# Layer norm, attention and a gated FFN on one core: the home and the request times of the down weights, and the order of work where two batches of the FFN meet

## The chip, the core and the metric

The kernel runs on one core of a Trainium2 chip. A core has five engines that run their own instruction queues side by side and meet only through semaphores: TensorE (PE in the profile; its weight loads are PEld), VectorE (DVE), ScalarE (ACT), GpSimd (POOL) and SyncE (SP). Transfers between the main memory and the on-chip memory are asked for by an instruction in the queue of SP, ACT or POOL; an instruction that waits holds up everything behind it in its queue. The metric is the time of one execution on the device, in microseconds (us). The kernel before was run three times: 1219.32, 1221.62 and 1223.13 us, so its median is 1221.62 us.

## The reference

```python
x = L0_attn_x                                  # (4, 512, 512), float32
xn = layernorm(x)
s = attention(xn)                              # 16 heads of 128, causal, with biases
g = silu(((silu((xn @ gate_w.T) * gate_s) * ((xn @ up_w.T) * up_s)) @ down_w.T) * down_s)
return x + s * g
```

There are four batches of 512 rows with 512 columns. `gate_w` and `up_w` are 1408 by 512, `down_w` is 512 by 1408. All data are float32. The weights of the FFN hold only the values -1, 0 and 1.

## The kernel before

The kernel has two stages. The first is the layer norm and the attention; its result for each batch and each tile of 128 rows goes to scratch tensors in main memory (`acc`), the last four of them from a tile `a_last` on chip (line 506). The second stage is the FFN with the final product (`ffn_exact`, lines 780 to 1106). A flag that is found during the first stage says whether the FFN weights are exact in the short form that TensorE multiplies; if so, `ffn_exact` runs. Each activation is split into a high and a low part (`hi`, `lo`), and each weight is multiplied with both.

The FFN cuts the 1408 inner columns into eleven chunks (`f` = 0 to 10). One chunk of one batch is a unit; the units go batch by batch, chunk by chunk. A unit is computed in one of two ways. In the plain way (`plain`) a gate product of 8 matmuls is followed by an up product of 8 matmuls, 512 columns each. The first four chunks of batch 0 and the first of batch 1 are plain (`PLAIN = (4, 1, 0, 0)`). All others use `seven` (lines 927 to 1002): a scheme of the Strassen kind, with seven products of 4 matmuls of 256 columns in place of the eight that two outputs need. It takes sums of the weights, made in the first stage and kept in main memory (`sum`), and sums of x, made on VectorE by `sums_of` (lines 806 to 853). `sums_of` has 13 additions on VectorE and 4 copies on ScalarE; it is a generator, and `advance(n)` lets the next n additions go into the queues. The four results are called t1 to t4, each as a high and a low part.

A unit is a list of (time, function). The functions of two neighbouring units are merged by their times: a unit starts every 7 steps and its functions run from step 0 to step 19. So the tail of a unit (`at9`, `at10`, `at11`, ...) is mixed with the head of the next (`at0`, `at1`, `at3`, ...). `run(upto)` issues everything due before a step. The names used below are: `at0` and `at1` are the two gate products (tiles px and py), with a ScalarE copy s1 after the first and a VectorE addition after the second; `at3` adds a product into px after s1 has been copied, then ScalarE copies u2 and applies silu; `at5` is the product s1 t1 into pz; `at6` adds into px again after u2 has been copied; `at8` is the VectorE addition c (tile `c22`) of pz and u3; `at9` and `at11` add the last products into px and pz. `at11` must wait until `at8` has read pz.

When the first unit of a new batch has been issued, the old batch gets its down product: for each of four tiles of 128 rows, 22 matmuls of 512 columns (`Down.add`, line 1025), and then `leave`: VectorE multiplies (line 766), ScalarE applies silu (767), VectorE multiplies by the attention's result and adds x (768, 769), SP stores. The down tiles have two PSUM buffers, so that the third tile starts only when line 766 of the first has run.

Buffers come from pools that are laid out on chip one behind the other in the order in which they are opened. The FFN's pools lie where the attention's pools lay. The first tile written in a pool waits for all users of everything that lay in that pool's whole range. Before, the order was: x sums (`tp`), the streamed weights (`fw`), the down weights (`wdp`), the inner activations (`hp`), the small temporaries (`fp`), the tail's inputs (`fa`). The range of `wdp` held, among others, a part of `a_last`.

All weights of the FFN are asked for by GpSimd's queue in program order (`load`, line 863; `load_down`, line 859). In each of the eleven units of batch 0 the unit's own weights come first and then one tile of down weights (line 1077).

Of the kernel before, what the change touches and what calls it, by code (L numbers as in the profile page):

```python
# [13 lines left out]
AF = mybir.ActivationFunctionType  # L14
# [29 lines left out]
def kernel(  # L44
# [69 lines left out]
    with ExitStack() as at:  # L114
# [464 lines left out]
        with tc.manual_schedule():  # L579
# [177 lines left out]
                    inexact = any_of(low)  # L757
            last = (NG - 1, B - 1)
            zs[last].append(attend(H - 1, pt, v_of[last], False))
            for t in range(NT):  # L760
                project_out(*last, t, zs[last])
            warm_up(LINGER)
# [17 lines left out]
    def ffn_exact():  # L780
        with ExitStack() as ff:

            tp = ff.enter_context(tc.tile_pool(name="tp", bufs=1))
            fw = ff.enter_context(tc.tile_pool(name="fw", bufs=3))
            wdp = ff.enter_context(tc.tile_pool(name="wdp", bufs=1))
            hp = ff.enter_context(tc.tile_pool(name="hp", bufs=NF + 1))
            fp = ff.enter_context(tc.tile_pool(name="fp", bufs=2))
            fa = ff.enter_context(tc.tile_pool(name="fa", bufs=3))
            ps_x = ff.enter_context(tc.tile_pool(name="ps_x", bufs=3, space=PSUM))
            ps_y = ff.enter_context(tc.tile_pool(name="ps_y", bufs=1, space=PSUM))  # L790
            ps_z = ff.enter_context(tc.tile_pool(name="ps_z", bufs=2, space=PSUM))
# [65 lines left out]
            def load_down(k):  # L857
                wd[k] = wdp.tile([P, D], F32R, name=f"wd{k}", tag=f"wd{k}")
                nc.gpsimd.dma_start(out=wd[k], in_=down_w[k])
# [66 lines left out]

            def seven(b, f):

                (b11, _), (b21, b22) = blk[b]
                t1, t2, t3, t4 = t_of[b]  # L930
                g = load(gate_w[f], [P, ND, P], "wg")
# [64 lines left out]
                def at17():  # L996
                    next(made["left"], None)

                return [
                    (0, at0), (1, at1), (3, at3), (5, at5), (6, at6), (8, at8), (9, at9),  # L1000
                    (10, at10), (11, at11), (13.5, at13), (15.5, at14), (17.5, at16), (19, at17),
                ]

# [35 lines left out]
            with tc.manual_schedule():  # L1039
                events, sums = [], sums_of(0)  # L1040

                def run(upto):

                    events.sort(key=lambda e: e[0])
                    while events and events[0][0] < upto:
                        events.pop(0)[1]()

                def advance(n=99):
                    for _ in range(n):
                        next(sums, None)  # L1050

                units = [(b, f) for b in range(B) for f in range(NF)]
                for k, (b, f) in enumerate(units):
                    at_ = 7 * k
                    if b > 0 and f == 1:

                        run(at_)
                        for e in [e for e in events if e[2] == k - 2]:
                            events.remove(e)
                            e[1]()  # L1060
                        if b == 1:
                            sums = sums_of(b)
                            advance()
                        for t in range(NT):
                            Down(b - 1, t).add(range(NF)).leave()
                            if t + 3 < NT:
                                load_tail(b - 1, t + 3)
                    if f < PLAIN[b]:
                        unit = plain(b, f)
                        if b == 0:  # L1070
                            advance((6, 3, 2, 1)[f])
                    else:
                        if b == 0 and f == PLAIN[b]:
                            advance()
                        unit = seven(b, f)
                    if b == 0:
                        load_down(f)
                    if 0 < b < B - 1 and f == 2:
                        sums = sums_of(b + 1)
                    if 0 < b < B - 1 and 2 <= f < 9:  # L1080
                        unit = sorted(
                            unit + [(2.5, lambda: advance(1)), (5.5, lambda: advance(1))],
                            key=lambda e: e[0],
                        )
                    events += [(at_ + n, what, k) for n, what in unit]
                    run(at_ + 7)
                    if f == NF - 1:
                        for t in range(3):
                            load_tail(b, t)
                last = B - 1  # L1090
                n0 = 7 * len(units)
                d0 = Down(last, 0).add(range(0, 4))
                run(n0 + 3)
                d0.add(range(4, 7))
                run(n0 + 6)
                d0.add(range(7, NF - 1))
                run(n0 + 99)
                d1 = Down(last, 1).add(range(NF - 1))
                d0.add([NF - 1]).leave()
                load_tail(last, 3)  # L1100
                d1.add([NF - 1]).leave()
                Down(last, 2).add(range(NF)).leave()
                h_ = D // 2
                d3 = Down(last, 3, slice(0, h_)).add(range(NF))
                d3.leave()
                Down(last, 3, slice(h_, D), nc.scalar, d3.o).add(range(NF)).leave()
# [175 lines left out]
```

## Time and profile before

| what | value |
|---|---|
| median of three runs | 1221.62 us |
| the profiled execution | 1221.51 us |
| span of its instructions | 1219.7 us |
| TensorE busy | 1194.8 us, 98% of the span |
| VectorE busy | 944.8 us, 77% |
| ScalarE busy | 599.8 us, 49% |
| GpSimd busy | 447.3 us, 37% |
| mean granted TensorE clock | 0.993 of full speed |
| FFN, from its first matmul to the end | 960.0 to 1219.7 us |
| main memory, read and written | 193 GB/s over the span |

The profile is of one execution. Its time is 1.8 us longer than the span between its first and its last instruction. "Busy" counts the time in which an engine had an instruction in hand; matmuls are pipelined, so that a small share of missing busy time can be the part that matters. "Granted clock" is the share of full speed that TensorE was allowed. A line such as "A <- B: 5.4, 1, 5.4" means that A waited for B 5.4 us in total, once, for 5.4 us at the longest.

### The profile page before, as it was taken

The page shows a single profiled execution, that of the slowest core. Times are in us where ns is not written, and L with a number is a line of the kernel's source. Part 1 is how long each engine was busy: PE and PEld are TensorE (multiplying, and loading weights), DVE is VectorE, ACT ScalarE, POOL GpSimd, SP SyncE. Part 2 cuts the span into 40 slices and gives each one's busy share as a digit, 9 for nine tenths or more (in the row PEclk, how much of TensorE's full clock was granted, in tenths as well). Part 3 has the DMA queues.
Part 4 walks back from the last instruction along what each step waited for, and adds up shares of the span by engine and source line. Part 5 has one row for each costly group of instructions (what it writes and reads, how often), then busy time and mean ns, then how long its engine had stood idle before and what let it go on. Part 6 is the DMA issues. An engine that isn't in the chain of part 4 may idle for free. (4 is left out here: it accounts for less than half of the span.)

```text
span 1219.7 us, 20216 instructions
## 1 busy us (share of the span) xinstructions
PE 1194.8 (98%) x6486; PEld 1040.9 (85%) x6486; DVE 944.8 (77%) x2496; ACT 599.8 (49%) x1449; POOL 447.3 (37%) x611
## 2 busy tenths in 40 slices
PE   9999999999999999999999999999999898999997
PEld 8888888888888888888888888888888697989896
DVE  7987777888778878787878787777777566859574
ACT  6654444554454445454545454455444252636362
POOL 3312342444244335333533354234322370525240
PEclk9999999999999999999999999999999898999999
DMA  4464456756676667666666666656555793959591
GB/s 162 144 188 151 144 177 194 216 173 213 200 215 191 210 202 227 191 206 201 201 199 190 199 206 205 208 184 183 173 156 165 249 334 98 290 155 290 147 272 55
DMA packets 133042, 236.75 MB, mean 194 GB/s; under 512 B 14912, under 2 KB 58688, under 8 KB 132928
## 3 DMA queue, kind: packets, MB, share of 16 engines
q1 hardware_dynamic: 77040, 140.15, 36.5%
q10 hardware_dynamic: 29520, 53.40, 14.7%
q0 software_dynamic: 26368, 41.82, 12.4%
q8 instruction: 54, 0.88, 0.3%
q14 instruction: 60, 0.49, 0.1%
HBM read 150.51 MB, written 84.80 MB: 193 GB/s over the span
## 5 line engine op out<-in xcount | busy, mean ns | idle before, releaser
L378 POOL TENSOR_SCALAR p<-p,rtot 128x512 f32<-128x512 f32 (+3 forms) x256 | 135.2, 547 | 566.3 <-DVE rtot L375 542.2
L372 ACT ACTIVATE p<-p,nmax 128x512 f32<-128x512 f32 (+3 forms) x256 | 140.9, 552 | 143.7 <-DVE nmax L358 143.7
L290 PE MATMUL psv<-wv,xh 128*128 128x512 f32 x448 | 124.7, 400 | 0.0
L106 PE MATMUL sc<-k,q 128*128 128x512 f32 (+2 forms) x576 | 112.6, 338 | 2.0 <-DVE xl L266 1.6
L392 DVE STREAM_TRANSPOSE sq<-p 128x256 f32<-128x256 f32 x378 | 113.4, 363 | 0.0
L106 PEld LDWEIGHTS sc<-k,q 128*128 128x128 f32 x576 | 99.0, 188 | 13.8 <-ACT xh L265 1.4
L315 ACT ACTIVATE k<-psk,consts 128x512 fp32r<-128x512 f32 (+1 forms) x65 | 44.3, 681 | 106.4 <-PE psk L106 106.3
L358 DVE CUSTOM_DVE_ANT_0 p<-sc,mask 128x512 f32<-128x512 f32 (+2 forms) x192 | 96.2, 550 | 0.0
L425 ACT CAST pt<-ptr 128x640 fp32r<-128x640 f32 x126 | 85.1, 724 | 10.7 <-DMA ptr<-turn 5.9
L427 POOL TENSOR_TENSOR pt<-ptr,pt 128x640 fp32r<-128x640 f32 x53 | 83.5, 1576 | 12.8 <-ACT pt L425 9.8
L290 PEld LDWEIGHTS psv<-wv,xh 128*128 128x128 f32 x448 | 76.0, 188 | 10.0
L316 DVE SCALAR_TENSOR_TENSOR k<-psk,consts,k 128x512 fp32r<-128x512 f32 (+1 forms) x65 | 48.1, 740 | 42.7 <-ACT k L315 42.2
L427 DVE TENSOR_TENSOR pt<-ptr,pt 128x640 fp32r<-128x640 f32 x73 | 76.6, 1060 | 2.6 <-ACT pt L425 2.6
L294 PEld LDWEIGHTS psv<-wv,xl 128*128 128x128 f32 x448 | 68.4, 188 | 9.5
L1025 PE MATMUL pd<-wd,hh 128*128 128x512 f32 (+1 forms) x187 | 71.6, 388 | 4.0 <-DVE o L766 4.0
L375 DVE RECIPROCAL rtot<-tot 128x1 f32<-128x1 f32 x256 | 41.4, 162 | 40.9 <-ACT p L372 34.7
L1025 PE MATMUL pd<-wd,hl 128*128 128x512 f32 (+1 forms) x187 | 71.3, 386 | 0.0
L294 PE MATMUL psv<-wv,xl 128*128 128x256 f32 x448 | 71.0, 280 | 0.0
L505 DVE TENSOR_TENSOR a<-pso,a 128x512 f32<-128x512 f32 x108 | 69.5, 684 | 1.4 <-DMA a<-acc 0.8
L315 ACT ACTIVATE q<-psq,consts 128x512 fp32r<-128x512 f32 (+1 forms) x65 | 44.2, 680 | 34.0 <-PE psq L106 33.7
L863 POOL DMA_DIRECT2D ws<-sum x78 | 41.6, 543 | 36.4 <-PE px L874 33.4
L863 POOL DMA_DIRECT2D wg<-in_gate_w x44 | 24.0, 546 | 78.2 <-PE py L874 68.1
(612 smaller groups left out, 3299.5 us busy)
## 6 DMA issues: line engine op xcount, KB each, us to landing
turn<-sq SPq DMA_DIRECT2D x63, 640.0 KB, 2.9
ptr<-turn SPq DMA_DIRECT2D x252, 160.0 KB, 5.2
acc<-a SPq DMA_DIRECT2D x124, 256.0 KB, 2.3
a<-acc ACTq DMA_DIRECT2D x108, 256.0 KB, 3.1
ws<-sum POOLq DMA_DIRECT2D x39, 384.0 KB, 4.7
wg<-in_gate_w POOLq DMA_DIRECT2D x44, 256.0 KB, 4.3
wu<-in_up_w POOLq DMA_DIRECT2D x49, 128.0 KB, 4.4
sum<-sums SPq DMA_DIRECT2D x22, 256.0 KB, 5.1
```

Source lines behind the costliest of these rows:

```text
L106: nc.tensor.matmul(ps, l, r, start=n == 0, stop=n == len(todo) - 1)
L290: nc.tensor.matmul(ps, x_[c].hi, wv[g].both[:, :, c, :], start=c == 0, stop=False)
L294: nc.tensor.matmul(ps[:, 1], x_[c].lo, wv[g].hi[:, c, :], start=False, stop=c == ND - 1)
L315: nc.scalar.activation(q.hi[:, at_], ps, AF.Identity, bias=bias[:, h : h + 1])
L358: nc.vector.tensor_tensor_reduce(out=of[t], in0=where[t], in1=add, scale=-SCALE, scalar=BIG, op0=ALU.add, op1=ALU.min, accum_out=nmax[t],)
L372: nc.scalar.activation(of[t], of[t], AF.Exp, bias=nmax[t], scale=-1.0, accum_out=tot)
L378: nc.gpsimd.tensor_scalar(of[t], of[t], rtot, 1.0, ALU.mult, ALU.mult)
L392: nc.vector.transpose(dst.rearrange("p a s i -> p s a i"), src.rearrange("p (s a i) -> p s a i", s=n, i=Q),)
L425: nc.scalar.copy(dst(pt.hi), src)
L427: on.tensor_tensor(dst(pt.lo), src, dst(pt.hi32), ALU.subtract)
L505: nc.vector.tensor_tensor(a, ps, a, ALU.add)
L1025: nc.tensor.matmul(self.ps, part, wd[f][:, self.c], start=f == 0 and part is h_.hi, stop=f == NF - 1 and part is h_.lo,)
```

## The change

Six edits, all but the first in `ffn_exact`:

1. At the end of the attention ScalarE runs one tiny activation with silu (`table(AF.Silu)`), after the last head's activations and before the last four output projections. ScalarE's function table for silu is then loaded there.
2. The pool of the down weights is opened last. So `hp`, `fp` and `fa` move down by its size, and the down weights lie behind them.
3. The down weights are asked for from the third unit of batch 0 on: one tile in the units 2 to 5, two in 6, one in 7 to 9, two in 10.
4. In the first `seven` unit of batches 0 and 1, `at5` is issued before `at3`.
5. In batch 1's x sums (`sums_of(1)`) five additions are issued ahead of batch 0's down tiles, then four behind each of the first two tiles (the third call finds nothing left), in place of all 13 ahead of the first tile.
6. Where two batches meet, `at8` of the new batch's first unit is issued ahead of the down tiles, and `at0` and `at1` of its second unit are issued between the third and the fourth down tile.

```diff
             zs[last].append(attend(H - 1, pt, v_of[last], False))
+            table(AF.Silu)
             for t in range(NT):
                 project_out(*last, t, zs[last])
...
             fw = ff.enter_context(tc.tile_pool(name="fw", bufs=3))
-            wdp = ff.enter_context(tc.tile_pool(name="wdp", bufs=1))
             hp = ff.enter_context(tc.tile_pool(name="hp", bufs=NF + 1))
             fp = ff.enter_context(tc.tile_pool(name="fp", bufs=2))
             fa = ff.enter_context(tc.tile_pool(name="fa", bufs=3))
+            wdp = ff.enter_context(tc.tile_pool(name="wdp", bufs=1))
...
-                    (0, at0), (1, at1), (3, at3), (5, at5), (6, at6), (8, at8), (9, at9),
+                    (0, at0), (1, at1), (3, at3), (2 if f == PLAIN[b] > 0 else 5, at5), (6, at6), (8, at8), (9, at9),
...
+                def at_once(which):
+                    for e in sorted(filter(which, events), key=lambda e: e[0]):
+                        events.remove(e)
+                        e[1]()
...
                         run(at_)
-                        for e in [e for e in events if e[2] == k - 2]:
-                            events.remove(e)
-                            e[1]()
+                        at_once(lambda e: e[2] == k - 2)
+                        at_once(lambda e: e[2] == k - 1 and e[1].__name__ == "at8")
                         if b == 1:
                             sums = sums_of(b)
-                            advance()
-                        for t in range(NT):
+                            advance(5)
+                        for t in range(NT - 1):
                             Down(b - 1, t).add(range(NF)).leave()
+                            if b == 1:
+                                advance(4)
                             if t + 3 < NT:
                                 load_tail(b - 1, t + 3)
...
-                    if b == 0:
-                        load_down(f)
+                    if b == 0 and f > 1:
+                        for n in range((f - 2) * NF // (NF - 2), (f - 1) * NF // (NF - 2)):
+                            load_down(n)
...
                     events += [(at_ + n, what, k) for n, what in unit]
+                    if b > 0 and f == 1:
+
+                        at_once(lambda e: e[2] == k and e[1].__name__ in ("at0", "at1"))
+                        Down(b - 1, NT - 1).add(range(NF)).leave()
                     run(at_ + 7)
```

## The prediction

> **What bounds the kernel now.** I read the page first: TensorE is busy for 98% of the span, and the FFN, which alone is changed, takes 960.0 to 1219.7 us. So only gaps in TensorE's queue, and a lowered clock behind them, can give time. Next the list of what TensorE waits for (us in total, times, longest):
>
> ```profile
> PE pg L874 <- DMA wg<-in_gate_w: 5.4, 1, 5.4
> PE pd L1025 <- DVE o L766: 4.0, 2, 3.7
> PE px L874 <- ACT s L953: 2.8, 4, 1.5
> PE pz L874 <- DVE c L949: 1.6, 2, 0.8
> ```
>
> Third, the chain of waits in order of time (start, us, what). It shows what each gap does to the matmuls behind it:
>
> ```profile
> 963.05 6.18 DMA wg<-in_gate_w
> 969.27 3.78 PE pg L874 x8
> ...
> 974.99 1.82 PE pg L874 x8
> ...
> 1025.12 13.10 PE pd L1025 x44
> ```
>
> Eight gate matmuls take 3.78 us behind the 5.4 us gap and 1.82 us when warm; 44 down matmuls take 13.10 us behind the 3.7 us gap where the first 44 took 9.98 (0.2268 each).
>
> Fourth, the timeline around each gap:
>
> ```profile
> 952.91 0.69 ACT L471 ACTIVATE z15h<-z,consts 128x512 fp32r<-128x512 f32 x1 [2.47 <-PE z L459]
> ...
> 962.53 0.53 POOL L859 DMA_DIRECT2D wd<-in_down_w  x1 [13.23 <-SPq L1278]
> 963.05 0.55 POOL L863 DMA_DIRECT2D wg<-in_gate_w  x1
> ...
> 984.31 0.36 ACT L953 COPY s<-px 128x256 f32<-128x256 f32 x1
> ...
> 1024.38 0.68 DVE L766 TENSOR_TENSOR o<-pd,ds_bc 128x512 f32<-128x512 f32 x1
> ...
> 1098.08 0.50 PE L874 MATMUL px<-xh,ws 128*128 128x256 f32 x2 [0.28 <-ACT s L953]
> ...
> 1099.61 0.50 PE L874 MATMUL pz<-xh,ws 128*128 128x256 f32 x2 [0.79 <-DVE c L949]
> ```
>
> GpSimd stands 13.23 us before the first down tile. Its semaphore waits in front of that load end at 962.0, when the last store of `a_last` (issued 959.8, 2.0 us to landing) is in: the pool of the down weights lies over `a_last`. Unit 1's gate weight is behind it in the queue, at 963.05, and lands at 969.23. At 1024.38 line 766 of the first down tile runs 8 us after its matmuls ended at 1016.3, behind 13 additions of x's sums.
>
> **What the skill says.** "TensorE: Matmul & The Clock Gate", Part 1: one idle window of about 3.4 us halves the clock, and about 3.4 us of work restores it. The trace agrees: gaps of 5.4 and 3.7 us were followed by slow matmuls, those of 1.5 us and less were not. "ScalarE: Activation LUTs", What ACT_TABLE_LOAD costs: 1283 ns and a drain of 1380. The trace has the 1283 ns but no drain: the cast ends at 963.00, the load starts at 963.01 and the silu at 964.31. "DMA: Bandwidth & Descriptors", Queues, rings and completion order: the DMA engines take turns between queues. The trace agrees: down tile, gate and up weights issued from 962.5 to 964 all landed after 5.6 to 6.2 us, beside 1.6 MB that SP asked for; those of 975 landed after 3.0 to 3.8.
>
> **The change, part by part.**
>
> *Start of the FFN (edits 1 to 4).* The first down load now stands behind unit 2's loads. So unit 1's weights no longer wait for 962.0. But the first weight of all gets a new wait: the built program lets it wait for the tiny silu, whose target lies in the range of `fw`. z15h ends at 953.60; table load 1.28 and activation 0.20 give 955.1 instead of the issue at 947.64. Behind it in GpSimd's queue are all loads of units 0 to 2. DMA moves 13 to 90 GB/s from 953.8 to 956.2, so I take 3.0 to 4.3 us to landing: 958.1 to 959.4, ahead of the gate product at 959.99. With the 6.7 us that this very load took in traffic it would be 961.8: a loss of 1.8. I take nothing. Unit 1's gate weight goes out about 957 and lands before 963.3 even at 6.2 us; it is needed at 963.7. Unit 3's must wait for GpSimd's step on up product 0 (962.9), then two loads and a down tile of 0.55 each: 964.5, landed by 970.7 at 6.2; needed at 971.0. Close; I take nothing here too.
>
> The wait for `a_last` does not vanish: the built program hands it to the first inner activation of `hp` (a ScalarE cast, about 965.2). It is over at about 962, so it is hidden by 3 us.
>
> TensorE then runs 8 products of 1.83: 960.0 + 14.65 = 974.65 for the first `seven`, where it was 982.09. That is 7.4 us earlier. What is late next is VectorE. It starts the sums at 960.17 as before, and all its work up to the first `seven` follows without a pause: six sums to 964.28 (silu now ready at 963.9, so the 0.58 us wait there goes), then per unit 1.56 from hd to hl, 0.61 on to the next, 0.69 per sum. hd of unit 1 at 968.5, of unit 2 at 972.1, of unit 3 at 975.0. Copy s1 comes 1.04 behind hh of unit 3 (as in the trace: 983.27 to 984.31), so at 976.95; the px product 0.42 later, 977.38, against 984.73. TensorE gets there at 974.65 + 3 x 0.48 = 976.1 (edit 4 brings `at5` ahead): 1.3 us of waiting, short enough for the clock. `at6` needs copy u2, 1.20 behind as before: 978.58 against 985.93. Gain 7.35; edit 4 alone is worth 0 to 0.5, since `at6` waits for u2 in either order.
>
> *Down loads (edit 3).* The same 11 issues of 0.557 us. Units with two ask GpSimd for 2.15 + 1.11 = 3.26 of a unit's 3.36 us. The seven `seven` units ask for 6.42 MB of their own (0.917 each) and 2.36 of down tiles: 8.78 MB in 23.5 us, 373 GB/s, against 340 moved in 985 to 1008, where TensorE had no load wait. The loads run up to 6 us ahead (968.2 against 974.65), so 300 GB/s will do. Cost 0; up to 2 us if that lead is used up.
>
> *Down tiles of batch 0 (edits 5, 6).* In the old clock, down starts at 1011.30 and the sums at 1015.45. Five sums at 0.69 bring line 766 of tile 0 to 18.83; the third tile needs it at 21.3. So the 3.68 us gap and the cold clock (13.10 - 9.98 = 3.1) go. From there VectorE: 766 to silu 0.71, to 768 0.66, to 769 0.73, to the next 0.61. Tile 0 done with 769 at 20.93; four sums; tile 1 at 24.21; four sums, the last one 0.8 for its copy; tile 2 at 29.66, silu 30.37, s1 copied at 31.25, sg at 32.4, tile 3's line 766 at 32.75. TensorE: 66 matmuls to 1026.28, `at0` and `at1` 0.96, 22 matmuls to 1032.24, `at5`, `at3` to 1033.2. Then `at6` wants u2, which stands behind tile 3's silu: 32.75 + 0.71 + 0.53 + 0.42 = 1034.4. It was 1041.11. Gain 6.7, with 1.2 us still waited. Bounds: 5 if VectorE slips another 1.7; 7.9 if it kept up.
>
> *Down tiles of batches 1 and 2 (edit 6).* Before, `at0` at 1096.21 and `at6` at 1100.67: 4.46 us for six products of 0.478 (2.87), so 1.59 lost; at 1155.80 to 1160.25 1.58. Now c has been added before the down tiles and s1 copied before the last. Behind that tile stand `at9`, `at3`, `at11`, `at5`; u2 is copied 0.20 + 0.72 + 0.54 after its end, and `at6` can go 0.41 later, 1.87 in all; the four products take 1.92. So nothing is waited; I take 1.5 each for both, 0.8 at the least.
>
> **Sum.** 7.35 + 6.7 + 2 x 1.5 = 17.05 us. Profiled execution 1221.51 - 17.05 = 1204.5, its span 1202.7 (1.8 lies around it); median 1221.62 - 17.05 = 1204.6.
>
> **Rivals.**
>
> *A, loads late at the start.* The new wait for silu, or unit 3's gate weight, makes TensorE wait again for 2 to 6 us, with the clock halved at the upper end. For it: margins of 0.6 to 1.9 us and 0.3 us at the worst latency. Against: DMA is nearly idle when the first is issued, and VectorE's pace hides 1.3 us of it. Time 1206.6 to 1210.6.
>
> *B, VectorE holds the seam of batches 0 and 1.* The sums between tiles delay tile 3's silu; if `at6` waits past 3.4 us the clock drops too. For it: 1.2 us is already waited in my sum. Against: tile 3's line 766 is due only 0.3 us behind its matmuls. Gain 3 there instead of 6.7: 1208.
>
> *C, the moved down loads starve batch 0: slower.* If DMA gave less than 8.78 MB in 23.5 + 6 + 17 = 46.5 us, that is below 189 GB/s, the `seven` units of batch 0 would give back the whole gain. Against: this stage moved 340 GB/s. At 180 GB/s the time is 1224.
>
> *D, the wait only changes its place.* Had `hp`'s first cast inherited a late store, ScalarE's silu of unit 1 would stand behind it, and the start would gain 3 at most: 1209. The store lands 3 us too early for that.
>
> **How the numbers follow.** My forecast (1202.5 to 1206.6) 0.63; A 0.17; B and D together 0.10 (1207 to 1210); more gain than counted, through VectorE keeping up at both seams (1201 to 1202.5), 0.05; C 0.02; between these and no change (1211 to 1225) 0.03. The range 1201.5 to 1210 leaves out little more than C, that remainder and the ends of A and B. A measurement of this kernel tells about 0.3% (3.7 us) from no change: faster 0.96, same 0.02, slower 0.02.
>
> **What would show it.** Right: no wait for wg on TensorE's list; the first `seven` at about 974.7 with a px wait of about 1.3 us on copy s; GpSimd's first weight at about 955.2; no table load behind 960; 88 down matmuls of batch 0 at 0.227 each; a 1.2 us wait for copy u behind them; no wait for c at the two later seams. Wrong: TensorE waiting for wg or wu near 960 or 971, a clock below 1.0 behind the first seam, load waits between 978 and 1003.

## The result, and the profile after

The changed kernel took 1206.78 us in the median of four runs (1206.35 to 1207.13), the kernel before, run beside it, 1220.93. The ratio is 0.9883 with a 95% interval of 0.9866 to 0.9900: about 14.2 us faster, where 17.05 had been predicted (1204.6). The profiled execution took 1206.52 us, its span 1204.7, at a mean granted clock of 0.999 (0.993 before).

The list of what TensorE waited for, after, in the FFN (us in total, times, longest):

```profile
PE px L875 <- ACT s L955: 2.1, 3, 1.1
PE px L875 <- ACT u L964: 1.5, 2, 1.1
...
PE px L875 <- DMA ws<-sum: 0.8, 2, 0.4
...
PE pd L1027 <- DVE o L767: 0.3, 1, 0.3
PE pg L875 <- ACT sg L912: 0.3, 1, 0.3
```

The 5.4 us for a gate weight and the 3.7 us for line 766 (now 767) are gone, and so is the wait for c. What stays are mostly waits for ScalarE's copies s and u. They are small, but two of the three for s are new in kind, as the last fence of this section shows.

Stage by stage, from the start of one matmul to the start of another in the two traces:

| stage | before | after | gain | predicted |
|---|---|---|---|---|
| first gate matmul to the first `at6` | 25.91 | 19.37 | 6.5 | 7.35 |
| to the first down matmul of batch 0 | 25.37 | 25.41 | 0.0 | 0 |
| first seam: to `at6` behind the down tiles | 29.81 | 23.10 | 6.7 | 6.7 |
| to the first down matmul of batch 1 | 35.12 | 35.43 | -0.3 | 0 |
| second seam: to `at3` of chunk 2 | 26.36 | 25.55 | 0.8 | 1.5 |
| to the first down matmul of batch 2 | 33.23 | 33.45 | -0.2 | 0 |
| third seam: to `at3` of chunk 2 | 26.35 | 25.55 | 0.8 | 1.5 |
| to the end | 57.6 | 57.7 | -0.1 | 0 |

The gains add up to 14.2 us. The spans differ by 15.0 us (1219.7 and 1204.7); the other 0.9 us lie ahead of the FFN, whose first matmul came at 959.11 instead of 960.02. Over all kernels of this document it comes at 958.70 to 961.30, so no edit is credited with that.

The start of the FFN in the timeline (start, us, engine, line, operation; in brackets the idle time before it and what ended it):

```profile
953.88 0.20 ACT L232 ACTIVATE junk<-eps 128x1 f32<-128x1 f32 x1
954.62 0.58 POOL L864 DMA_DIRECT2D wg<-in_gate_w  x1 [8.29 <-ACT junk L232]
...
964.14 0.54 POOL L864 DMA_DIRECT2D wg<-in_gate_w  x1
...
964.90 0.62 ACT L886 CAST hh<-hd 128x512 fp32r<-128x512 f32 x1 [1.60 <-DMA fx<-in_x]
...
970.92 1.16 PE L875 MATMUL pg<-xh,wg 128*128 128x512 f32 x4 [0.33 <-ACT sg L912]
...
977.28 0.50 PE L875 MATMUL px<-th,ws 128*128 128x256 f32 x2 [1.05 <-ACT s L955]
```

GpSimd's first weight waits for the tiny silu and goes out at 954.62. It lands in time. Unit 3's gate weight (964.14) took 6.7 us and landed at 970.8, and gate product 3 starts at 970.92. It was due 3.63 us behind gate product 2, at 970.12, so it is 0.8 late. The bracket names ScalarE's `sg`, which ended at about the same time; but that is the silu of gate product 2, and the gate products have three PSUM buffers, so product 3 doesn't need it. Where the releaser that is named can't be the one by the code, look for a transfer that has just landed.

The first seam in the chain of waits:

```profile
1004.05 14.96 PE pd L1027 x66
1019.01 0.47 PE px L875 x4
1019.48 0.48 PE py L875 x4
1019.96 5.03 PE pd L1027 x22
...
1026.02 0.02 issue
1026.05 0.63 ACT o L768
1026.67 0.27 ACT u L964
```

66 down matmuls in 14.96 us are 0.2267 each: no gap and no slow clock. At the end of the seam the path leaves TensorE for the fourth tile's silu (line 768) and the copy u behind it.

The second seam in the timeline:

```profile
1085.70 0.69 DVE L770 TENSOR_TENSOR o<-o,fx 128x512 f32<-128x512 f32 x1
...
1086.70 0.41 DVE L951 TENSOR_TENSOR sg<-pz,u 128x256 f32<-128x256 f32 x1
...
1087.15 0.51 ACT L896 ACTIVATE sg<-sg,consts 128x256 f32<-128x256 f32 x1 [0.69 <-DVE sg L951]
...
1087.56 0.35 ACT L955 COPY s<-px 128x256 f32<-128x256 f32 x1
...
1087.97 0.50 PE L875 MATMUL px<-xh,ws 128*128 128x256 f32 x2 [0.54 <-ACT s L955]
```

Here is the new wait. VectorE works through the fourth tile's lines 769 and 770 in order, then reaches sg of chunk 1; ScalarE waits 0.69 us for it in order to apply silu; copy s of chunk 2 stands behind that silu; and TensorE waits 0.54 us for s. The same happens at the third seam.

### The profile page after: what moved, and what is told of

Read it like the earlier page. It is cut to its first block, busy times and chain, and to the rows that moved or that the text cites. A ratio compares the mean times of both kernels' runs of the same rounds, so it can differ in the third digit from the quotient of the medians.

```text
span 1204.7 us, 20215 instructions
## 1 busy us (share of the span) xinstructions
PE 1187.9 (99%) x6486; PEld 1036.3 (86%) x6486; DVE 946.5 (79%) x2496; ACT 599.6 (50%) x1450; POOL 449.1 (37%) x611
## 5 line engine op out<-in xcount | busy, mean ns | idle before, releaser
L459 PE MATMUL z<-pt,v_0h 128*128 128x512 f32 x128 | 50.6, 395 | 0.0
```

## The experiments

Twelve kernels were run, in three groups, each beside the kernel before (medians there 1221.38, 1221.42 and 1221.28 us). Stage times are from the profiled execution of each; the first two columns of interest are the start (first gate matmul to first `at6`) and the first seam (first down matmul to `at0` of chunk 2, a mark that all kernels have).

| kernel | median us | ratio to before, 95% | start | first seam |
|---|---|---|---|---|
| before (profile) | 1221.4 | | 25.9 | 30.38 |
| changed | 1206.78 | 0.9866 to 0.9900 | 19.37 | 23.67 |
| e8, edit 3 alone | 1214.04 | 0.9927 to 0.9960 | 18.72 | 29.17 |
| e7, edit 2 alone | 1216.89 | 0.9946 to 0.9974 | 22.17 | 30.44 |
| e2, edit 2 undone | 1207.13 | 0.9867 to 0.9900 | 18.92 | 23.67 |
| e3, silu's target apart | 1207.02 | 0.9869 to 0.9902 | 18.46 | 23.69 |
| e1, edits 5 and 6 undone | 1214.78 | 0.9935 to 0.9968 | 18.74 | 29.08 |
| e5, edit 5 undone | 1212.30 | 0.9911 to 0.9944 | 18.82 | 28.97 |
| e10, edit 6 undone | 1209.35 | 0.9878 to 0.9911 | 18.76 | 24.56 |
| e9, tail inputs later | 1209.88 | 0.9891 to 0.9924 | 18.93 | 23.68 |
| e4, fourth leave later | 1211.49 | 0.9913 to 0.9949 | 19.21 | 23.08 |
| e11, fourth leave split | 1206.20 | 0.9863 to 0.9915 | 19.30 | 23.68 |
| e12, and its store apart | 1205.43 | 0.9856 to 0.9894 | 19.15 | 23.68 |
| e13, and s first | 1204.64 | 0.9849 to 0.9882 | 17.67 | 23.68 |

The start stage scatters: 18.7 to 19.4 us in the eight kernels that have the changed kernel's program there (changed, e1, e2, e4, e5, e10, e11, e12; e2 apart from the home). The time from gate product 2 to gate product 3 goes with it, 3.63 us where nothing waits:

| | e3 | e8 | e9 | e1 | e10 | e5 | e2 | e12 | e4 | e11 | changed |
|---|---|---|---|---|---|---|---|---|---|---|---|
| gate 2 to gate 3 | 3.63 | 3.63 | 3.63 | 3.85 | 3.91 | 3.94 | 3.97 | 4.21 | 4.26 | 4.37 | 4.43 |
| start stage | 18.46 | 18.72 | 18.93 | 18.74 | 18.76 | 18.82 | 18.92 | 19.15 | 19.21 | 19.30 | 19.37 |

With the changed kernel's start, unit 3's gate weight makes gate product 3 late by 0.2 to 0.8 us from one execution to another (it lands 0.1 to 0.4 us before that product starts in each of these traces), and what exceeds some 0.2 us reaches the first `at6`. Differences of a few tenths between these kernels in that column are not read as effects of an edit.

### Which edit carries the start

**e8_requests_only**: the kernel before with edit 3.

```diff
-                    if b == 0:
-                        load_down(f)
+                    if b == 0 and f > 1:
+                        for n in range((f - 2) * NF // (NF - 2), (f - 1) * NF // (NF - 2)):
+                            load_down(n)
```

> The kernel before with edit 3 alone: down tiles asked for from the third chunk on; their home, the silu table, at5's place and both seams are the kernel before's. Theory (the requests alone carry the start): first gate matmul to the first at6 19 to 20 us (before 25.91, changed 19.37), no wait of TensorE for wg of 5 us, seams 29.8 to 30.4 and 27.8 as before: about 1214.8. Rival (the home, the table load or at5's place is needed as well: the down tile's wait for a_last still holds units 2 and 3, or the table load behind the first gate product delays VectorE's chain): stage of 21 us or more, 1216.5 or later.

Measured: 1214.04 us, start stage 18.72, no wait for wg. The first theory holds, and more sharply than it was put: with edits 1, 2 and 4 absent the stage is shorter than in the changed kernel (19.37). The silu table is still loaded behind the first cast, as the timeline of this kernel shows:

```profile
962.04 1.28 ACT L911 ACT_TABLE_LOAD   x1
...
963.40 0.53 POOL L859 DMA_DIRECT2D wd<-in_down_w  x1
```

The first down tile is asked for at 963.40, without a wait: `a_last` is in by then, so the old home costs nothing. The late table costs little. In this trace VectorE waits 0.57 us for the first silu, and from there to copy s, for which TensorE waits, it waits only for ScalarE's hh and never for TensorE. In e3 below, where the table comes early and no weight is late, VectorE doesn't have that wait, but waits 0.31 us for TensorE's up product 3 instead. So about 0.26 us are left, which is what stands between 18.72 here and 18.46 there. Edit 4 adds nothing in this stage: `at6` starts 1.21 us behind the product of `at3` in both, with `at5` between them here and ahead of them there.

**e2_old_home**: the changed kernel, `wdp` opened where it was before.

```diff
             fw = ff.enter_context(tc.tile_pool(name="fw", bufs=3))
+            wdp = ff.enter_context(tc.tile_pool(name="wdp", bufs=1))
             hp = ff.enter_context(tc.tile_pool(name="hp", bufs=NF + 1))
...
-            wdp = ff.enter_context(tc.tile_pool(name="wdp", bufs=1))
```

> The changed kernel with the down weights' pool in its old place (edit 2 undone, edit 3 kept). My theory: the home by itself decides little, since with edit 3 the first down load comes at 963.6, when a_last is nearly stored; GpSimd then waits up to 1.2 us for the last store and unit 3's gate weight comes that much later, while the first cast of hp no longer waits: 0 to +1.2 us against the changed kernel, 1206.8 to 1208. Rival: the home is what removed the wait, and its loss brings the 5.4 us gap and the slow clock back: 1213 or more.

Measured: 1207.13 us, within the spread of the changed kernel. GpSimd waits 1.4 us ahead of the first down tile, and TensorE does not notice. Given edit 3, the home is worth nothing.

**e7_home_only**: the kernel before with edit 2 (`wdp` opened last, requests as before).

```diff
-            wdp = ff.enter_context(tc.tile_pool(name="wdp", bufs=1))
...
             fa = ff.enter_context(tc.tile_pool(name="fa", bufs=3))
+            wdp = ff.enter_context(tc.tile_pool(name="wdp", bufs=1))
```

> The kernel before with edit 2 alone: the down weights' pool opened last, the requests still one tile behind each unit's weights from the first unit on. Theory (home and requests are two ways to the same end, and the requests are the better one): the first down tile now waits only for the last output projection's matmul near 958.9, not for a_last's last store near 962.0; unit 1's gate weight goes out near 959.5 where it is needed at 963.7, so TensorE waits 0 to 2 us for it, and the stage from the first gate matmul to the first at6 takes 20 to 21.5 us (before 25.91, requests alone 18.72): about 1216.5. Rival (the home does nothing by itself): 25 us or more, 1221. Other rival (it is as good as the requests): under 19.5, 1214.

Measured: 1216.89 us, start stage 22.17 where 20 to 21.5 was expected. The mechanism is as put: the first down tile goes out at 958.45 and unit 1's gate weight at 958.97, and TensorE waits 1.84 us for that weight. The size missed for another reason. The matmul that waited, and then the trace in windows (window, its length, busy time of PE, PEld, DVE, ACT, POOL with instructions, then granted clock, DMA share, GB/s):

```profile
964.63 1.81 PE L874 MATMUL pg<-xh,wg 128*128 128x512 f32 x4 [1.84 <-DMA wg<-in_gate_w]
```

```profile
961.55:964.96 3.41, 1.57 (x7) 1.00 (x6) 2.42 (x5) 2.80 (x5) 1.76 (x5) 1.00 1.14 318
964.96:968.37 3.41, 3.41 (x9) 2.64 (x8) 2.59 (x4) 0.97 (x3) 0.45 (x1) 0.50 1.16 380
```

The clock fell to half behind a wait of 1.84 us and stayed there for 3.41 us, which costs about 1.7 us; without them the stage would have taken some 20.5 us (an estimate from these figures). This was the slowest of the five runs of this kernel (1218.71; the others 1216.48 to 1216.93). So home and requests are two ways to the same end. Alone, the home is worth 4.4 us and the requests 7.4 (medians; in the profile of e8 7.2 of them at the start).

**e3_junk_apart**: the changed kernel, with the tiny silu writing to a tile outside `fw`'s range.

```diff
-            table(AF.Silu)
+            nc.scalar.activation(const.tile([P, 1], F32, name="junk_c"), eps, AF.Silu)
```

> The changed kernel, but the tiny silu writes to a tile of its own that no FFN pool covers. My theory: the first weight load then goes out 7 to 8 us earlier, 0.8 MB leave the crowd of transfers from 954.6 to 965, the last store of a_last lands before 963.5 and unit 3's gate weight sooner, so that the waits of 0.3 us (first cast of hp) and 0.5 us (gate product of unit 3) go: first gate product to first at6 18.6 us in place of 19.4, time 0.8 us under the changed kernel. Rival: the crowd is made by SP's loads for the tail, issued 959.5 to 962.9; then unit 3's gate weight still takes over 6 us and at most 0.3 us is gained.

Measured: 1207.02 us. The first weight went out at 948.01 instead of 954.62. hh no longer waited for `a_last`, gate product 3 came without a wait, and the stage took 18.46 us, as the first theory has it. But 0.28 came back in batch 0's `seven` units (25.69), and a gain in time, 0.8 us by the theory, is not shown. So the wait on silu that edit 1 brings is what crowds unit 3's weight and the stores, at a price below what these runs can tell.

**e9_tail_late**: the changed kernel, with the six tail inputs of batch 0 moved from SyncE at 959.5 us to ScalarE's queue in chunks 6 to 8.

```diff
+                    if b == 0 and 6 <= f < 9:
+                        load_tail(0, f - 6, nc.scalar)
-                    if f == NF - 1:
+                    if b > 0 and f == NF - 1:
                         for t in range(3):
                             load_tail(b, t)
```

> The changed kernel with the six tail inputs of batch 0 (1.6 MB, asked for by SyncE from 959.5 us on) asked for by ScalarE's queue in chunks 6 to 8 instead. Theory (they are the crowd that made a_last's stores take up to 5.9 us and unit 3's gate weight 6.7 us): the stores land after 2 to 3 us, the first hh cast no longer waits, unit 3's gate weight lands after 3 to 4.5 us, gate product 3 doesn't wait, and the start stage is 0.5 us shorter (18.85 where the changed kernel had 19.37): about 1206.3. Rival (VectorE's chain to copy s sets the stage anyway): transfers are quicker, but the wait of px for s grows from 1.05 to about 1.5 us and the stage stays at 19.3: 1206.8; the six issues on ScalarE may cost it 0.3 more.

Measured: 1209.88 us, 3 us slower than the changed kernel: neither theory gives that. At the start, gate product 3 no longer waited (3.63 us behind the second), as the first theory has it, and px waited 1.5 us for s instead; the stage came to 18.93. But `a_last`'s stores still took up to 6.2 us and hh still waited for them, until 965.03. The tail inputs were not the crowd that held the stores; in e3, where the seven weight loads of units 0 to 2 went out 6.6 us earlier, the stores took 2.0 to 2.8 us and hh did not wait. They were the crowd for unit 3's gate weight, which landed after 3.2 us here. The price was paid in batch 0's `seven` units, 28.30 us instead of 25.41. About half of it is a late weight, batch 1's first gate weight:

```profile
PE pg L875 <- DMA wg<-in_gate_w: 1.2, 1, 1.2
```

The other half, about 1.4 us, is ScalarE's queue: in each of the chunks 6 to 8 two issues of tail inputs stand ahead of a copy s, and px waits for it. The first of the three places in the timeline:

```profile
986.47 0.37 ACTq L1012 DMA_DIRECT2D fx<-in_x  x1
...
987.37 0.51 PE L875 MATMUL px<-th,ws 128*128 128x256 f32 x2 [0.41 <-ACT s L955]
```

The late weight took 7.5 us from issue to landing where the changed kernel's took 5.8, and there it landed 0.85 us before it was needed (998.40 and 999.25): that is the room that edit 3 leaves at this place. This was not a bound on the rate as such. From 978 to 1003.9 us the transfers moved 358 GB/s here and 341 in the changed kernel. The Trainium skill, "DMA: Bandwidth & Descriptors", Specifications, gives about 358 GB/s as the main memory's limit for one core, but e5 below moved more over 15 us:

```profile
961.90:976.90 15.00, 13.91 (x68) 11.28 (x66) 11.32 (x22) 6.85 (x15) 12.03 (x23) 1.00 1.27 387
```

So 358 GB/s was not the limit in these runs, and why this stretch of e9 went no faster stays open.

### Which edit carries the seams

**e1_no_seams**: the changed kernel with edits 5 and 6 undone.

```diff
-                        at_once(lambda e: e[2] == k - 1 and e[1].__name__ == "at8")
-                            advance(5)
-                        for t in range(NT - 1):
+                            advance()
+                        for t in range(NT):
                             Down(b - 1, t).add(range(NF)).leave()
-                            if b == 1:
-                                advance(4)
...
-                        at_once(lambda e: e[2] == k and e[1].__name__ in ("at0", "at1"))
-                        Down(b - 1, NT - 1).add(range(NF)).leave()
```

> The changed kernel with edits 5 and 6 undone, so the edits at the start of the FFN alone (1 to 4). My theory: the start gives 6.6 us of the 14.2 by itself, so from the first gate product to the first at6 it takes 19.4 us (25.9 before), and the first seam of batches takes 29.8 us again: time about 1214.3. Rival: part of the seam's gain was made by the start (weights that run further ahead): then the first seam stays under 28 us and the time is below 1212.5.

Measured: 1214.78 us. The 3.7 us wait for line 767 is back, and both 0.8 us waits for c. Up to `at6` the seam took 28.50 us where 29.8 was expected; the last section shows why.

**e5_sums_first**: edit 5 undone alone (`advance()` in place of `advance(5)`).

```diff
-                            advance(5)
+                            advance()
```

> The changed kernel with edit 5 undone alone: all 13 additions of batch 1's x sums ahead of batch 0's down tiles, edit 6 kept. Theory (edit 5 is what frees the first seam): the wait of the third down tile for line 767 of the first returns with about 3.7 us and the slow matmuls behind it with about 3; from the first down matmul to the gate product of the unit two further on about 29 us (changed kernel 23.67, both edits undone 29.08), so 5 to 5.5 us lost: about 1212. Rival (edit 6 carries the first seam too, since it puts two products ahead of the last tile): the stage stays near 24.5 us, 1207.6.

Measured: 1212.30 us, first seam 28.97, and on TensorE's list:

```profile
PE pd L1027 <- DVE o L767: 4.0, 2, 3.7
```

The first theory holds: edit 5 is worth 5.5 us, and without it edit 6 does next to nothing at this seam (28.97 against e1's 29.08).

**e10_no_six**: edit 6 undone alone, the sums still spread.

```diff
-                        at_once(lambda e: e[2] == k - 1 and e[1].__name__ == "at8")
-                        for t in range(NT - 1):
+                        for t in range(NT):
...
-                        at_once(lambda e: e[2] == k and e[1].__name__ in ("at0", "at1"))
-                        Down(b - 1, NT - 1).add(range(NF)).leave()
```

> The changed kernel with edit 6 undone alone: edit 5's spread sums are kept, but at8 and the next unit's at0 and at1 stand behind all four down tiles, as before. Theory (edit 6 is worth 0.7 us at each seam and no more: it takes away a 1.6 us wait for c and brings one of 0.8): first down matmul to at0 of chunk 2 about 24.7 us at the first seam (23.67 with edit 6), the later seams 24.9 + 6.72 instead of 23.4 + 7.51, about 1209.2. Rival (edit 5 needs edit 6, because the sums between the tiles push the fourth tile's silu and the copies behind it): 26 us or more at the first seam, 1211 or later.

Measured: 1209.35 us, first seam 24.56, the later ones 24.9 + 6.72 instead of 23.4 + 7.51 us. The first theory holds. Edit 6 is worth 2.6 us in the runs, and in the profiles 0.9 at the first seam and 0.7 at each later one.

### What the new wait at the later seams is

**e4_leave_late**: the whole `leave` of the fourth tile is issued at step 8.5 of the next unit instead of directly behind its matmuls.

```diff
-                        Down(b - 1, NT - 1).add(range(NF)).leave()
+                        d_last = Down(b - 1, NT - 1).add(range(NF))
+                        events.append((at_ + 8.5, d_last.leave, k))
```

> The changed kernel, but what follows the fourth down tile's matmuls at each seam (multiply, silu, multiply, add, store) is issued 8.5 steps into the unit, behind the next unit's first copies. My theory: the waits behind the fourth tile are made by this work standing in the queues of ScalarE and VectorE: the 1.06 us wait for copy u at the first seam and the 0.54 us waits for copy s at the two later ones (0.75 us each from start to start) go, about 2.5 us less: 1204.3. Rival: VectorE has no room in the units behind, and the same work makes other products wait: 1206 to 1208.

Measured: 1211.49 us, 4.7 slower than the changed kernel. Half of the theory holds: the later seams themselves got shorter, 24.79 us each instead of 25.55. But the rival holds too, and costs more than it was given. The timeline behind the second seam:

```profile
1091.53 0.69 DVE L769 TENSOR_TENSOR o<-o,fa 128x512 f32<-128x512 f32 x1 [0.69 <-ACT o L768]
...
1095.14 0.51 PE L875 MATMUL px<-xh,ws 128*128 128x256 f32 x2 [1.15 <-ACT s L955]
```

Issued in one piece, `leave` makes VectorE stand 0.69 us for ScalarE between lines 767 and 769. With its three operations that is 2.8 us in the middle of units that have no such room, and px waits up to 1.15 us for s. In this execution the clock also halved at the start of batch 0's `seven` units, behind waits of 1.05 and 0.46 us that the changed kernel has as well (26.90 us there instead of 25.41; the edit doesn't touch this stage).

**e11_split_leave**: lines 767 and 768 of the fourth tile stay; 769 and 770 take the places of two of the next x sums, which begin one chunk later; the store goes with 770.

```diff
-                        Down(b - 1, NT - 1).add(range(NF)).leave()
+                        d_last = Down(b - 1, NT - 1).add(range(NF))
+                        nc.vector.tensor_tensor(o_, d_last.ps, ds_bc, ALU.mult)
+                        nc.scalar.activation(o_, o_, AF.Silu)
+                        events += [(at_ + 9.5, left_a, k), (at_ + 12.5, left_x, k)]
...
-                    if 0 < b < B - 1 and f == 2:
+                    if 0 < b < B - 1 and f == 3:
                         sums = sums_of(b + 1)
-                    if 0 < b < B - 1 and 2 <= f < 9:
+                    if 0 < b < B - 1 and 3 <= f < 10:
```

> The changed kernel; of the fourth down tile's leave, the first multiply and silu stay where they are, but its second multiply, its addition and its store are issued at steps 9.5 and 12.5 of the unit, in the places of two of the next x sums, which begin one chunk later. Theory (the new wait of 0.54 us at the later seams is copy s, which stands on ScalarE behind silu of sg1, which waits for VectorE behind just these two operations): the wait goes at both later seams, at0 of chunk 2 to at0 of chunk 4 takes 6.72 us again instead of 7.51, 1.5 us in all: about 1205.2. Rival (VectorE has no room in those units either, as when the whole leave was moved): waits of 0.5 to 1 us for s or u two units later, 1206.8 or later.

Measured: 1206.20 us; from `at0` of chunk 2 to that of chunk 4 it took 6.73 and 6.83 us at the later seams instead of 7.51. The stages of the later seams took 24.84 us instead of 25.55. The cause of the new wait is thereby shown. The gain did not all arrive, though: the last stage (from `at0` of chunk 4 of batch 3 to the last matmul) took 46.66 us instead of 45.59. The timeline of this kernel in batch 3:

```profile
1149.16 0.33 SPq L1110 DMA_DIRECT2D out<-o  x1
1149.54 0.42 SPq L1010 DMA_DIRECT2D fa<-acc  x1
...
1162.10 0.51 PE L875 MATMUL px<-xh,wg 128*128 128x256 f32 x2 [0.81 <-DMA wg<-in_gate_w]
```

In SyncE's queue the next batch's six tail inputs stand behind the late store. They went out from 1149.5 to 1153.6 us, where the changed kernel has them from 1145.8 to 1149.6, and a gate weight was 0.81 us late.

**e12_store_apart**: e11 with that store in ScalarE's queue, some steps behind line 770.

```diff
-                            d.store.dma_start(out=out[d.b, ts(d.t, P), :], in_=d.o)
+                        def left_o(d=d_last):
+                            nc.scalar.dma_start(out=out[d.b, ts(d.t, P), :], in_=d.o)
```

> The kernel with the split leave, its store asked for by ScalarE's queue two steps behind the addition instead of by SyncE. Theory (with the split leave the late store held the six tail inputs of the next batch behind it in SyncE's queue, 1149.5 to 1153.6 instead of 1145.8 to 1149.6, and these took the DMA engines from a gate weight that came 0.81 us late): SyncE asks for four of them ahead of the fourth tile's end, no wait for wg, both later seams 6.72 and the last stage 45.6: about 1205.0. Rival (the wait for wg comes from something else, or the two tail inputs that need the fourth tile's buffers still collide): the last stage stays at 46.5, 1206.2.

Measured: 1205.43 us, last stage 45.64, no wait for wg. Four of the six inputs now go out from 1139.7 to 1141.6, under the down tiles. The theory holds in the trace; the medians of e11 and e12 differ by 0.8 us, and their runs overlap (1205.89 to 1211.35, and 1204.72 to 1208.77).

**e13_s_first**: e12, and at batch 0's first `seven` the copy s goes ahead of the last plain unit's cast hh and of the last sum's cast.

```diff
-                return [(1, gate), (5, up)]
+                if b == 0 and f == PLAIN[0] - 1:
+                    return [(1, gate), (5, up), (7.5, leave)]
+                return [(1, gate), (5, up)]
...
-                        if b == 0 and f == PLAIN[b]:
-                            advance()
                         unit = seven(b, f)
+                        if b == 0 and f == PLAIN[b]:
+                            unit = sorted(unit + [(0.6, advance)], key=lambda e: e[0])
```

> The kernel with the split leave and the store apart, and at batch 0's first seven the copy s goes on ScalarE ahead of the last plain unit's cast hh and of the last x sum's cast, instead of behind both. Theory (the 1.05 us that px waits for s at the start, and the time that at6 then waits for u, stand on these two casts of 0.53 us and on nothing else): the wait for s falls from 1.05 to 0.3 or less, the start stage to 17.8 to 18.5 us (18.7 to 19.4 in the kernels so far), about 1204.1. Rival (VectorE's lateness sets it: sg0, hl and the last sum are then the late ones, or at6 waits longer for u or for xl): the stage stays at 18.7 or more, 1205.

Measured: 1204.64 us, start stage 17.67. The timeline:

```profile
974.71 0.37 ACT L962 COPY s<-px 128x256 f32<-128x256 f32 x1 [1.38 <-PE px L875]
...
976.68 0.50 PE L875 MATMUL px<-xh,ws 128*128 128x256 f32 x2 [0.57 <-ACT u L971]
...
998.23 0.77 PEld L875 LDWEIGHTS pg<-xh,wg 128*128 128x128 f32 x4 [0.28 <-DMA wg<-in_gate_w]
```

The wait for s is gone altogether. But batch 0's `seven` units took 26.31 us instead of 25.41: the second half of `at6` now waits 0.24 us for VectorE's last sum xl, as the rival had it, and one weight load at their end waits for its transfer. Of 1.5 us gained against e12 at the start, 0.9 is lost there, and the medians differ by 0.8 in all (their runs overlap). All four runs of e13 (1204.16 to 1205.97) lie under all four of the changed kernel (1206.35 to 1207.13). It is the best version here, by about 2.1 us, and both are compared with the kernel before in different groups.

## Why the prediction was right or wrong, point by point

**The start (7.35 predicted, 6.5 in the profile).** The path was right: weight at 955.2 (954.62), no wait for wg at the first gate, px waiting about 1.3 us on s (1.05), `at6` 1.20 behind (1.20). Two margins that were taken at nothing did cost. The step "Unit 3's ... needed at 971.0. Close; I take nothing" failed by 0.8 us: TensorE started at 959.11 rather than 960.0, so the product was due at 970.12, and the transfer took 6.7 us where 6.2 had been taken; hd of unit 3 then came 0.48 us late to VectorE. And the step that hid `a_last`'s store by 3 us took its end from the trace of before (about 962), though the weights that move to 954.6 share the engines with it: its last store landed at 964.7, and hh went 0.3 us late. Rivals A and D both happened, each with under a microsecond. Where neither acts, in e3, the stage took 18.46 us; the sum had 25.91 - 7.35 = 18.56. The mechanism was right, and the two margins are the terms that were mis-sized. That the first `seven` came at 974.64, where 974.65 stood in the sum, is luck: TensorE started 0.9 us early and lost 0.8 to the weight. One reading behind these margins was too kind: the loads of 975.4 and 975.9 did land after 3.0 and 3.2 us before, but those of 976.4 to 978.0 after 5.1 to 5.5, with nothing of SyncE's beside them. GpSimd's own loads crowd one another.

What the prediction had wrong in kind is the credit. It gave the start to edits 1 to 4 together. Edit 3 does it alone (e8). The home is another way to a part of it, and worth nothing beside edit 3. Of the 0.58 us that the early table was to give VectorE, 0.26 are seen in e3 against e8; in the changed kernel the wait that comes with the table makes unit 3's weight late and takes it back (18.7 to 19.4 us in the kernels with its start, 18.72 in e8). That edits 3, 5 and 6 alone would make the changed kernel's time follows from these runs, but such a kernel was not run.

**The first seam (6.7 predicted, 6.71).** Put on the new clock (down starts at 1003.89 instead of 1011.30), the sum said 1025.34 for the fourth tile's multiply and 1026.99 for `at6`; the trace has 1025.33 and 1026.99. Following VectorE's queue operation by operation was exact here. e5 and e10 divide it: edit 5 takes away the gap and the slow clock, edit 6 adds 0.9 us.

**The later seams (1.5 each predicted, 0.8).** The step that failed is "So nothing is waited". It followed ScalarE's silu and u copy of chunk 1 and stopped there. Lines 769 and 770 also stand in VectorE's queue, ahead of sg of chunk 1; silu of that sg stands in ScalarE's ahead of s of chunk 2; and TensorE wants that s 0.54 us earlier. One look further along both queues would have shown it. e11 shows the cause: with these two operations out of the way the stage is 24.84 us, 1.5 below the 26.36 before, which is the gain that the sum had. The lower bound of 0.8 held.

**The rest (0 predicted, -0.7).** The four stages between grew by 0.04 to 0.3 us each; two waits of 0.4 us for `ws`, in batches 1 and 2, make up most of it. Kernels with the same program in these two stages (e1, e2, e3, e5, e8, e9, e10) show 35.07 to 35.53 and 33.24 to 33.73 us there, so this is about what one execution differs from another.

**Rival C, starved loads.** "300 GB/s will do" was right for the changed kernel, which moved 341 with no load wait in this stage. It was nearer to the edge than the 180 GB/s of the rival made it look, by the lead of single weights: 0.85 us at the end of the stage, and e9 used it up with 1.6 MB more to move.

**Rival B** did not happen: 1.06 us waited where 1.2 was in the sum. The forecast's part that "1.3 us of waiting [is] short enough for the clock" held for the profiled execution. It depends on where the wait falls: see the last section.

The 17.05 became 14.2 by 0.8 at the start, 1.4 at the later seams and 0.7 in the stages between.

## What to carry to other kernels

When a piece of work is moved in an in-order queue, follow what stands behind it until the chain meets an engine that has slack: here the wait went from VectorE through ScalarE's silu to a copy of the next unit, one step beyond where the working stopped, and moving the piece whole (e4) or its store (e11) made new waits behind it. A request that waits needn't be given a better place in memory if it can be made later, at a time when it no longer waits. And a stage whose matmuls never wait may still have little lead in its transfers (0.85 us here): what is moved into it (e9), or what makes it start sooner (e13), can be paid back in part in late weights.

## What the runs showed of the hardware that was not expected

- The granted clock changed only on a grid. In each of the 14 traces, the times at which it rose or fell while the kernel ran lie whole multiples of 3.413 us apart. In e7 it fell at 964.96, rose at 968.37, fell at 1019.57 and rose at 1026.40: 1, 16 and 18 steps from the first. The Trainium skill, "TensorE: Matmul & The Clock Gate", Part 1, says that the clock is set by an activity window of about 3.4 us that is free-running and doesn't start with the kernel; the traces agree. The page lets the clock fall after an idle window. Here a window that was about half idle was enough. Laid on the grid, over all traces, a window at full speed in which TensorE was busy for 1.57 us or less was always followed by half speed, and one with 1.83 us or more kept full speed, but for one of 1.91 us in e4. So waits add up within a window, and their place decides: those of 1.05 and 0.46 us fell into one window in e4 and halved the clock, and into two in the changed kernel (busy 2.58 and 2.73 us), where nothing happened. In e9 waits of 1.51 and 0.46 us left a window with 1.90 us, and the clock held.
- How long the half speed lasts depends on the grid too. The same 3.68 us gap at the first seam was followed by 6.83 us at half speed (14 slow matmuls) before and in e7, and by 3.41 us (7 to 9) in e1, e5 and e8. Windows of the kernel before, and then one of e1:

```profile
1024.29:1027.70 3.41, 2.58 (x6) 2.11 (x7) 2.68 (x5) 0.63 (x1) 0.00 (x0) 0.50 0.00 0
1027.70:1031.12 3.42, 3.42 (x9) 2.65 (x9) 1.46 (x3) 0.63 (x1) 0.00 (x0) 0.50 0.76 271
```

```profile
1017.56:1020.98 3.42, 3.27 (x8) 2.60 (x9) 2.08 (x4) 1.21 (x2) 0.00 (x0) 0.50 0.10 38
```

  The gap reached 0.83 us (e7: 0.69) into the first window at half speed, which was then busy for only 2.58 us (e7: 2.72), and a second window followed. In e1 it reached 0.15 us into it, in e5 and e8 it was over, and one window was all. This is what stands between 30.4 and 29.0 to 29.2 us at that seam in the table. The grid lies differently in each execution (the first rise comes 4.26 to 7.22 us into the span), so it need not have to do with an edit; that one and the same kernel has both lengths is not shown, with one trace of each.
- A transfer of 256 KB took 4.1 us to land when few others were under way (the first gate weight), 6.7 us beside the down tile, the tail inputs and the stores; stores of the same size went from 2.0 us before to 5.9 after, because the weight loads had moved to their time (in e3, where these go out earlier, the last three took 2.0 us again).
